# Unread matmuls in shorter pauses of TensorE, placed nearer to the next step

## The chip, the cores and the metric

The kernel runs on one core of one Trainium2 chip. The metric is the time of one execution on the device in microseconds; lower is better. All times in this text are from this kernel on that chip. Times of the profile are counted from the start of its span.

## The reference

The input x has 8 sequences of 1024 rows of 256 numbers. Four stages follow each other, each with a residual sum around it and a layer norm in front:

1. A linear attention layer with 16 heads of width 16: q and k are sigmoids of projections, two rounds of running sums over the sequence give the flows that scale them, and kv is a running sum of outer products. A projection, a layer norm, a dense layer of width 1024 with GELU and a second layer norm belong to the stage.
2. A dense layer of width 1024 with ReLU.
3. Softmax attention over the whole sequence with width 256.
4. A gated feed-forward layer of inner width 704 whose inputs and weights are first rounded, in blocks of 16, to a grid of eight magnitudes (FP4) times a scale per block.

Cut to its last lines:

```python
    x = x + _L0_attn_ref(_layernorm(x, axis=-1), ...)
    x = x + _L0_ffn_ref(_layernorm(x, axis=-1), ...)
    x = x + _L1_attn_ref(_layernorm(x, axis=-1), ...)
    x = x + _L1_ffn_ref(_layernorm(x, axis=-1), ...)
```

All matmuls are in float32; one such matmul stands in the trace as two passes, each with its own weight load. A transpose against the identity is one pass.

## The kernel before, in words

The work is cut into 64 chunks of 128 rows. Four chunks are a group, two groups a sequence, so there are 16 groups p. `linear_group` (L998) and `linear_span` (L1061) do the linear attention of a group, `dense` (L1451) the two dense layers, `soft_chunk` (L1620) the softmax attention and the FP4 layer of one chunk, `fp4_weights` (L787) the rounding of the weights. A chunk is turned by `flip` (L683) either on TensorE against the identity or by a copy on GpSimd (`cut`), a transposing DMA (`spun`) and a copy on ScalarE. Group 0 goes through TensorE, and in its case in two halves.

Each of these functions is a Python generator. It yields what its next step needs (an engine, tiles, a number of PSUM banks) and issues instructions when it is resumed. All generators lie in one list, and `Plan.run` (L330) chooses which one goes on. The order of instructions on every engine is then fixed as the order in which they were issued. So the program's order is set at build time by estimates of time:

- `Plan.took` (L176) holds a cost for each operation, and books when its engine is free again and when each tile is ready and last used. For TensorE it also books `ran`, the estimated end of the last matmul (L246). A pause of over 2.0 us in the estimates doubles the cost of the matmuls of the next 2.1 us (L242 to L246).
- `Plan.ready` (L298) answers when the step's engine is free and when its tiles and banks are there. `banks_free` (L126) tells from when on a number of the 8 PSUM banks can be had.
- `Plan.run` takes the step with the smallest key: first how long TensorE would wait for it, last its place in the plan (due times from the table `T` at L31).
- When the chosen step is TensorE's and the estimates leave a pause on TensorE before it, `run` may call `fill` (L1774). It takes one PSUM bank and issues products of the identity with itself into it. Nobody reads them. Their number is set at build time; on the chip they stand in TensorE's queue like any matmul, and what stands behind them waits until they are done. The first of them can run only when GpSimd has made the identity (`make_identity`, L497).

In the kernel before, such products are put where the estimated pause is over 1.6 us and a bank is free within 0.4 us of the pause's start; their estimated length is the pause less 0.7 us, at 0.22 us each. The estimate of the first pause counts from 0, since `ran` starts at 0 (L110).

All instructions are issued through one helper (L376), so the profile shows L376 for nearly all of them. They are told apart by their tiles: `bank<-ident` are the unread products, `bank<-ident,n` and the like are transposes.

Of the kernel before, what the change touches and what calls it, by code (L numbers as in the profile page):

```python
# [75 lines left out]
class Plan:  # L76
# [253 lines left out]
    def run(self):  # L330
        while self.parts:
            now = self.free.get("tensor", 0.0)
            best = None
            for part in self.parts:
                t = self.ready(part[1])
                if t is None:
                    continue
                stays = self.tiled and part[1].tiled
                queue = part[1].queue
                wait = max(max(t) - now - (0.3 if stays or part[2] < 0.0 else 0.0), 0.0)  # L340
                urgent = part[2] < 0.0
                unripe = 0.0 if urgent else max(t[1] + self.RIPE[queue] - now, 0.0)
                key = wait, unripe, queue == "tensor", not stays, part[2]
                if best is None or key < best[0]:
                    best = key, part, max(t)
            assert best is not None, "every part waits for another"
            pause = max(now, best[2]) - self.ran
            if pause > 1.6 and best[1][1].queue == "tensor" and self.fill is not None:
                if (self.banks_free(best[1][1].banks + 1) or 0.0) <= self.ran + 0.4:
                    self.fill(pause - 0.7)  # L350
            if best[0][0] > 0.0 or best[1][1].queue == "tensor":
                self.free["tensor"] = max(now, best[2])
            part = best[1]
            need = next(part[0], None)
            if need is None:
                self.parts.remove(part)
            else:
                part[1] = need
                if need.at is not None:
                    part[2] = need.at  # L360
# [34 lines left out]
def block_stack_kernel(ctx: ExitStack, tc: tile.TileContext, a: dict, out: bass.AP):  # L395
# [20 lines left out]
    plan = Plan(tc, tc.nc)  # L416
# [16 lines left out]
    def mm_bank():  # L433
        bank = ps.tile([P, 512], F32, tag="bank", name="bank")
        plan.bank(bank)
        return bank
# [1334 lines left out]
            )  # L1771
            plan.start(soft_chunk(cc), T["soft"] + min(cc, B * NCH - T["tail"]) / 4)

    def fill(us):  # L1774

        bank = mm_bank()
        while us > 0.0:
            nc.tensor.matmul(bank[:, :P], lhsT=ident, rhs=ident, start=True, stop=True)
            us -= 0.22
        plan.let_go(bank)  # L1780

    plan.fill = fill
# [45 lines left out]
```

## Time and profile before

| What | us |
|---|---|
| median of 3 timed runs | 2479.97 (2478.25 to 2480.6) |
| the profiled execution | 2475.61 |
| its span, first to last instruction | 2473.9 |
| TensorE (PE) busy | 2431.3 |
| VectorE (DVE) busy | 1893.8 |
| ScalarE (ACT) busy | 1397.6 |
| GpSimd (POOL) busy | 1233.7 |
| unread products: 310 passes, busy | 39.6 |

PE is TensorE's matmul row and PEld its weight loads. Matmuls are pipelined, so that a row's end is modelled and reaches some 0.16 us into the row that follows it back to back. A row of the timeline gives start, length, engine, line, operation, output and inputs, shape and number; brackets behind it give the idle time of that engine just before, and what ended it. The mean granted clock of TensorE is 0.996 of full speed over the span.

### The profile page before, as it was taken

Reading aid. Unit: us, or ns where it says so; the run is one execution under the profiler, and the core shown is the slowest. Engines: PE = TensorE matmul, PEld = TensorE weight load, DVE = VectorE, ACT = ScalarE, POOL = GpSimd, SP = SyncE. Lnnn points to the kernel's source line nnn. Section 1 sums busy time; section 2 is a strip of 40 time slices with the busy share of each in tenths; the row PEclk is TensorE's granted clock in tenths of the full one; section 3 lists DMA queues with packets and bytes.
Section 4 is the critical chain, followed back from the end, with each engine's and each line's share of the span. In section 5 each row is a group of like instructions: output and inputs, shape, how many; then the busy total and the mean of one; then the engine's idle time right before and its main releaser. Section 6 shows DMA issues by size and latency. Waiting matters only on the chain.

```text
span 2473.9 us, 47678 instructions
## 1 busy us (share of the span) xinstructions
PE 2431.3 (98%) x16503; PEld 1896.0 (77%) x16503; DVE 1893.8 (77%) x4139; ACT 1397.6 (56%) x2913; POOL 1233.7 (50%) x2257
## 2 busy tenths in 40 slices
PE   8899999999999999999999999999999999999998
PEld 6787777777777777777777777777777777777766
DVE  6877687967868788786977878787786877766777
ACT  5444556465565556656466565555556555555454
POOL 3354546454554646455563555546455464544342
PEclk9999999999999999999999999999999999999999
DMA  3265455555455556564555465556554655555242
GB/s 103 71 155 155 125 145 129 143 139 137 114 122 150 130 128 145 131 133 121 149 137 129 114 151 127 129 136 131 134 137 125 145 119 130 126 122 131 68 83 56
DMA packets 630354, 312.62 MB, mean 126 GB/s; under 512 B 433760, under 2 KB 618592, under 8 KB 630112
## 3 DMA queue, kind: packets, MB, share of 16 engines
q1 hardware_dynamic: 630112, 309.57, 51.5%
q8 instruction: 131, 2.15, 0.4%
q14 instruction: 111, 0.91, 0.1%
HBM read 188.17 MB, written 20.71 MB: 84 GB/s over the span
## 4 chain that ended last, share of the span: by engine, by line
PE 88%; DVE 7%; DMA 2%; ACT 1%; POOL 1%; issue 1%; SPq 0%; DVEq 0%; ACTq 0%; POOLq 0%
PE bank L376 88%; DMA spun<-cut 1%; DVE hid L376 1%; DVE prod L376 1%; DVE u L376 0%; DVE n L376 0%; DVE ln_st L376 0%; DVE x_amax L376 0%; POOL ln_rstd L376 0%; DVE w_raw L376 0%; DVE res L376 0%; POOL cut L376 0%; DVE div L376 0%; POOL ln_shift L376 0%; DVE ln_mv L376 0%
## 5 line engine op out<-in xcount | busy, mean ns | idle before, releaser
L376 PE MATMUL bank<-half,w_in 128*128 128x256 f32 x2048 | 532.2, 383 | 12.5 <-ACT half L376 7.9
L376 PE MATMUL bank<-w_out,hidden 128*128 128x256 f32 x2048 | 524.3, 384 | 2.6 <-DMA w_out<-in_L_attn_W_dram 1.9
L376 PEld LDWEIGHTS bank<-w_out,hidden 128*128 128x128 f32 x2048 | 378.0, 190 | 104.5 <-issue 46.3
L376 PEld LDWEIGHTS bank<-half,w_in 128*128 128x128 f32 x2048 | 385.8, 191 | 83.7 <-issue 13.2
L376 POOL TENSOR_SCALAR ln_ve<-ln_mv 128x1 f32<-128x1 f32 x384 | 101.3, 264 | 560.8 <-DVE ln_mv L376 520.9
L376 ACT ACTIVATE hidden<-bank,c_L_attn_b 128x256 f32<-128x256 f32 x256 | 120.2, 470 | 242.7 <-PE bank L376 242.4
L376 ACT ACTIVATE hidden<-bank,c_L_ffn_b 128x256 f32<-128x256 f32 x256 | 121.1, 473 | 236.8 <-PE bank L376 235.4
L376 POOL TENSOR_TENSOR ln_rstd<-ln_ve,neghalf 128x1 f32<-128x1 f32 x384 | 232.3, 605 | 32.0
L376 PE MATMUL bank<-n2T,qT 128*128 128x512 f32 x512 | 242.0, 596 | 2.5 <-ACT qT L376 2.5
L376 PE MATMUL bank<-vt,probT 128*128 128x256 f32 x1024 | 231.9, 379 | 0.0
L376 POOL COPY cut<-n 128x512 uint16<-128x512 uint16 x238 | 170.9, 726 | 96.7 <-DVE n L376 58.0
L376 PEld LDWEIGHTS bank<-vt,probT 128*128 128x128 f32 x1024 | 193.5, 190 | 31.9 <-issue 5.3
L376 POOL COPY cut<-hid 128x512 uint16<-128x512 uint16 x165 | 117.6, 736 | 154.3 <-DVE hid L376 133.9
L376 POOL COPY cut<-prob 128x512 uint16<-128x512 uint16 x218 | 145.7, 691 | 93.9 <-ACT prob L376 54.2
L376 PE MATMUL bank<-wdT,hqT 128*128 128x256 f32 x768 | 177.3, 380 | 1.8 <-ACT hqT L376 1.8
L376 PE MATMUL bank<-wgT,xqT 128*128 128x352 f32 x512 | 173.9, 462 | 1.6 <-ACT xqT L376 1.2
L376 PE MATMUL bank<-wuT,xqT 128*128 128x352 f32 x512 | 172.4, 459 | 0.0
L376 ACT COPY probT<-spun 128x512 uint16<-128x512 uint16 x246 | 159.2, 673 | 19.9 <-DMA spun<-cut 19.6
L376 ACT ACT_TABLE_LOAD x128 | 164.2, 1283 | 3.7 <-PE bank L376 1.5
L376 PEld LDWEIGHTS bank<-wdT,hqT 128*128 128x128 f32 x768 | 144.8, 190 | 26.9 <-ACT hqT L376 3.2
L376 PEld LDWEIGHTS bank<-n2T,qT 128*128 128x128 f32 x512 | 97.0, 191 | 74.7 <-issue 59.2
L376 PEld LDWEIGHTS bank<-wuT,xqT 128*128 128x128 f32 x512 | 97.3, 190 | 54.2
(274 smaller groups left out, 4808.1 us busy)
## 6 DMA issues: line engine op xcount, KB each, us to landing
w_in<-in_L_attn_W_dram SPq DMA_DIRECT2D x128, 256.0 KB
w_out<-in_L_attn_W_dram SPq DMA_DIRECT2D x128, 256.0 KB
w_in<-in_L_ffn_w_dram SPq DMA_DIRECT2D x128, 256.0 KB
w_out<-in_L_ffn_w_dram SPq DMA_DIRECT2D x128, 256.0 KB
spread<-packed SPq DMA_DIRECT2D x90, 256.0 KB
spun<-cut SPq DMA_TRANSPOSE x767
x<-in_L_attn_inputs_dram SPq DMA_DIRECT2D x64, 128.0 KB
xr<-in_L_attn_inputs_dram SPq DMA_DIRECT2D x64, 128.0 KB
```

The source lines that it names most:

```text
L376: ins = method(*args, **kw)
```

## The change

Three things in `run` and `fill`:

- Products are now put into estimated pauses of over 0.9 us, before 1.6 us.
- They are to end 0.4 us before the next step, before 0.7 us. `fill` gets this point in time in place of a length, and `run` sets `ran` to it.
- While nothing has run on TensorE (`ran` is 0), the pause is counted from 2.4 us on, and a product is reckoned as 0.36 us. Else it is reckoned as 0.22 us, as before.

The condition on the bank is the same. The estimates in `took` are the same, but each product passes through them, so the planner's later choices could differ.

```diff
-            pause = max(now, best[2]) - self.ran
-            if pause > 1.6 and best[1][1].queue == "tensor" and self.fill is not None:
+            until = max(now, best[2])
+            if until - self.ran > 0.9 and best[1][1].queue == "tensor" and self.fill is not None:
                 if (self.banks_free(best[1][1].banks + 1) or 0.0) <= self.ran + 0.4:
-                    self.fill(pause - 0.7)
+                    self.fill(until - 0.4)
+                    self.ran = until - 0.4
             if best[0][0] > 0.0 or best[1][1].queue == "tensor":
                 self.free["tensor"] = max(now, best[2])
...
-    def fill(us):
+    def fill(until):
 
         bank = mm_bank()
+        us = until - (plan.ran or 2.4)
+        each = 0.22 if plan.ran else 0.36
         while us > 0.0:
             nc.tensor.matmul(bank[:, :P], lhsT=ident, rhs=ident, start=True, stop=True)
-            us -= 0.22
+            us -= each
         plan.let_go(bank)
```

## The prediction

> **What bounds the kernel now.** The page's first view gives the busy shares, its fourth the chain that ended last. I then read TensorE's own timeline for its pauses, the windows view for the granted clock beside them, and the two built programs' orders of instructions for where products come and go.
>
> ```profile
> PE 2431.3 (98%) x16503; PEld 1896.0 (77%) x16503; DVE 1893.8 (77%) x4139; ACT 1397.6 (56%) x2913; POOL 1233.7 (50%) x2257
> ...
> PE 88%; DVE 7%; DMA 2%; ACT 1%; POOL 1%; issue 1%; SPq 0%; DVEq 0%; ACTq 0%; POOLq 0%
> ```
>
> TensorE is the chain for 88% of the span and stands idle for only 2473.9 - 2431.3 = 42.6 us. So a product that nobody reads is free only inside a real pause; between two matmuls that already follow each other it is paid in full. A fill can earn time in two ways only: TensorE starts earlier, or its clock stays up.
>
> The orders show what the diff becomes. There were 155 unread products in 13 places; there are 240 in 30. The first place falls from 25 to 10; the others grow from 130 to 230, that is 100 more. All other TensorE instructions keep their order, SP and POOL are the same, and DVE and ACT differ by one or two neighbours exchanged, which I price at nothing. No DMA is moved. One product is two passes; 28 passes from 2452.31 to 2455.44 give 0.112 us each, so **0.223 us a product** at full clock.
>
> **Part 1, the start.** TensorE's and DVE's timelines:
>
> ```profile
> 3.10 8.46 PE L376 MATMUL bank<-ident 128*128 128x128 f32 x50 [3.10 <-POOL ident masks.py:199]
> 11.39 0.60 PE L376 MATMUL bank<-ident,n 128*128 128x128 f32 x4
> ...
> 7.22 0.41 DVE L376 TENSOR_SCALAR n<-x,ln_mv,ln_rstd 128x256 f32<-128x256 f32 x1 [0.44 <-POOL ln_rstd L376]
> ...
> 11.66 0.18 DVE L376 BATCH_NORM_AGGREGATE ln_mv<-ln_st 128x2 f32<-128x6 f32 x1
> 14.18 0.69 DVE L376 TENSOR_TENSOR_SCAN prod<-one,k 128x256 f32<-128x256 f32 x1 [2.34 <-ACT k L376]
> ```
>
> The second normalised chunk is ready at 7.22 + 0.41 = 7.63, but its transposes wait behind 50 unread passes until 11.39. Seen from 5.60 on, 39 passes are left, so 11 took 2.50 us (0.227 each, half clock); 20 passes then end at 3.10 + 20 x 0.227 = 7.6. The transposes go some 3.7 us earlier. What is late next is DVE: it runs without a pause until 11.66 + 0.18 = 11.84, and its scan, which waited 2.34 us for ACT's k, can start there and not sooner. Later DVE waits on ACT (0.17, 0.90 us) give back a little more. I take **-2.6**; bounds -1.0 (the 16 passes of wk and wq at half clock, 16 x 0.22 = 3.5 us more, partly inside the 1.56 us of fill that follows them) and -3.5.
>
> **Part 2, the clock.** The windows view, laid at the edges where the granted clock changes:
>
> ```profile
> 30.40:35.90 5.50, 1.93 (x21) 1.11 (x20) 4.68 (x11) 2.08 (x9) 2.90 (x4) 1.00 0.08 25
> 35.90:42.73 6.83, 5.77 (x8) 2.47 (x9) 3.69 (x7) 3.10 (x7) 0.72 (x1) 0.50 0.44 114
> 114.41:117.82 3.41, 1.52 (x28) 1.05 (x29) 3.19 (x9) 1.77 (x3) 1.36 (x2) 1.00 0.00 0
> 117.82:121.23 3.41, 3.41 (x10) 2.75 (x9) 1.46 (x5) 3.27 (x9) 0.00 (x0) 0.50 0.03 7
> 209.98:213.39 3.41, 1.36 (x6) 1.24 (x7) 3.12 (x11) 0.95 (x3) 2.33 (x6) 1.00 0.52 121
> 213.39:216.81 3.42, 3.42 (x9) 2.72 (x9) 2.41 (x6) 1.31 (x4) 1.72 (x4) 0.50 0.66 199
> 247.53:250.94 3.41, 2.02 (x18) 1.82 (x16) 3.24 (x12) 1.60 (x5) 1.06 (x4) 1.00 0.92 202
> ```
>
> Columns: stretch, length, busy time of PE, PEld, DVE, ACT, POOL, granted clock, DMA. After a stretch in which PE was busy 35 to 45% (1.93 of 5.50, 1.52 and 1.36 of 3.41) the next one has half the clock; after 59% (2.02 of 3.41) it has not. At 612.75 to 616.17 (0.61 of 3.42) the fourth such spell begins.
>
> *The spell at 35.90.* Four passes of n2T,wk take 3.78 us there and 1.88 at 46.77; those of wq 2.63 and 1.98; the transposes before 0.69 and 0.44. Together 1.90 + 0.65 + 0.25 = 2.8. Behind them DVE stands:
>
> ```profile
> 39.41 0.28 DVE L376 TENSOR_TENSOR scale<-e,div 64x128 f32<-64x128 f32 x1
> ...
> 45.05 0.75 DVE L376 TENSOR_TENSOR q<-q,bank 128x256 f32<-128x256 f32 x2 [4.70 <-PE bank L376]
> ```
>
> Scale is ready at 39.69 and TensorE reaches it at 43.79, so 2.8 fit into those 4.1. Nine new products (2.0 us) lie before the hsum and total matmuls; they bring the stretch to (1.93 + 2.0)/5.50 = 71% busy. I take **-2.8**, bounds 0 and -2.8.
>
> *The spell at 213.39.* Five products go into the 2.37 us pause before 212.03: (1.36 + 1.12)/3.41 = 73%. The 12 passes from 212.03 take 3.98 us to the next start; at 0.216 (four in 0.86 at 1164.66) they take 2.6. **-1.4**, bounds 0 and -1.4; the DMA that follows (w_in, released by the last of them) moves with it.
>
> *The other spells.* No fill is put before the one at 616.17, and in front of 117.82 only 2 products are added, ahead of the pauses. I leave both. The 2.82 us pause at 249.5 gets 6 more products; it caused no spell here, so on the profiled execution it earns nothing.
>
> A rule weighed against this: the Trainium skill, "TensorE: Matmul & The Clock Gate", section "HAM oscillation — how this bites in real kernels", tells writers to avoid idle gaps of over about 3.4 us. By it no pause of this kernel needs a fill, both spells would stay, and the sum below would be +4.8. The rows above speak against it: the pauses before the spells were 2.37 us and less, and what they share is a low busy share. Its section "What's actually happening" says that the 3413 ns window runs free, which agrees with the 3.41 and 6.83 us lengths here.
>
> **Part 3, products in front of ready work.** Two places from TensorE's timeline:
>
> ```profile
> 1164.66 1.03 PE L376 MATMUL bank<-half,w_in 128*128 128x256 f32 x4
> 1165.52 1.03 PE L376 MATMUL bank<-w_out,hidden 128*128 128x256 f32 x4
> ...
> 2349.94 0.81 PE L376 MATMUL bank<-ident,prob 128*128 128x128 f32 x4
> 2351.47 1.98 PE L376 MATMUL bank<-n2T,qT 128*128 128x512 f32 x4 [0.71 <-ACT qT L376]
> ```
>
> Six products go between the first two, which have no pause: +1.34. The others on the chain: 5 at 121.6 (+1.12); 3 at 160.6, where 0.25 us was idle (+0.42); 5 at 696.3 (+1.12); 3 at 739.8 (+0.67); 5 at 2338.7 and 4 at 2350.8, 2.01 less the 0.71 idle (+1.30); 5 at 2447.1, in front of the last wgT matmuls whose result DVE's last chunk waits for (+1.12). That is 36 products, less the two pauses: **+7.1**. From 616 to 1354 the chain is TensorE without a break, so nothing there absorbs them. The rest is covered and I take **+0.3** for all: 1 to 6 more each at 16, 18, 26.7, 62.5, 98, 105, 110, 133.6, 219.2, 252, 279, 338, 1527, 2424, 2452 and 2459, where TensorE at its next waits stands for 0.2 to 2.8 us (on DVE, ACT or DMA), and 4 each at 61 and 2467 in pauses of 0.2 to 0.6 us. If that cover were gone, their price would be the remaining 100 - 36 - 9 - 5 = 50 products, +11 us. Lower bound for all of part 3: half, +3.7, if DVE has slack behind some of them.
>
> **Sum** against the profiled execution (2475.6 us, span 2473.9): -2.6 - 2.8 - 1.4 + 7.1 + 0.3 = +0.6. That execution is 4.4 us under the median of the timed runs (2479.97). Two or three more spells of 3.41 us at half clock, 1.7 us each, would make such a difference, and a pause causes one or not by where it falls in the window. The pause at 249.5 would cause one in about 6 of 10 executions (it must leave some 1.8 us of a 3.41 us window idle); filled, that is -1.0 against the median. Forecast: 2480.0 + 0.6 - 1.0 = **2479.6**.
>
> **Rivals.** *Faster.* The start gains 3.5, the spell at 117.82 falls away too with the changed phase (-1.7), and half of part 3 is absorbed by DVE's slack: -3.5 - 2.8 - 1.4 - 1.7 - 1.0 + 3.7 = -6.7, 2473.3. For it: DVE is busy 77% and has stretches of its own on the chain (598 to 616, 1354 to 1378). Against it: PE's timeline has no idle time over 0.2 us from 620 to 1378, so there is no slack to take from.
>
> *Slower: the fills do not hold the clock.* If the new products around 32 to 36 us leave a free-running window below about half busy, the spell there stays, and fills inside it cost double. Then parts of 2 give 0, the 5 products at 121.6 lie in a half-clock spell (+1.1) and the total is -2.6 + 7.4 + 1.1 = +5.9, 2485.9. It decides at a busy share between the 45% that lost the clock and the 59% that kept it; the 1.23 us pause before 36.50 stays unfilled, so a window around it can come to about 50%.
>
> *The change does nothing measurable at its places* (each fill exactly replaces idle time, the clock as before) is inside the forecast's range.
>
> **How the numbers follow.** Bounds of the parts, not all at once: low -6.7, high +5.9. Chances: forecast 0.66, the faster rival 0.21, the slower one 0.13. 0.2% is 5.0 us, about what a measurement of this kernel can tell from no change. The range that should hold 8 in 10 goes from 2473.4 to 2485.4; the forecast's own is 2475 to 2485.
>
> **What would show it.** Right: 20 unread passes from 3.10 and transposes by 8; DVE's first scan near 11.9; a granted clock of 1.00 from 36 to 43 and n2T,wk in some 1.9 us; no spell after the pause that was at 209.7; and rows of 6 to 12 unread passes at about 690, 735 and 1160 with no idle time before or after. Wrong: wk at half clock after the start, the 6.83 us spell still there, or an idle pause of TensorE right after a fill in the steady part, which would mean that the fill cost nothing. The forecast fails if the clock gains and the product costs do not come to nearly the same size, or if an unread product waits for its bank.

## The result, and the profile after

| | before | after |
|---|---|---|
| median of the timed runs, us | 2477.89 (12 runs, 2472.9 to 2480.6) | 2485.91 (12 runs, 2483.9 to 2489.2) |
| the profiled execution, us | 2475.61 | 2485.57 |
| its span, us | 2473.9 | 2483.9 |
| PE busy, us | 2431.3 | 2448.4 |

The change makes the kernel slower: 1.0039 of the time before, with a 95% interval of 1.0031 to 1.0047. By the medians that is +8.0 us. The forecast was no measurable change. Its starting point, 2480.0, was the median of three runs; the 12 runs here put the kernel before 2.1 us lower. The page of the changed kernel, busy time and chain:

```profile
PE 2448.4 (99%) x16673; PEld 1915.3 (77%) x16673; DVE 1892.9 (76%) x4139; ACT 1397.0 (56%) x2913; POOL 1234.6 (50%) x2257
...
PE 88%; DVE 6%; DMA 1%; POOL 1%; ACT 1%; issue 1%; SPq 0%; POOLq 0%; DVEq 0%; ACTq 0%
```

TensorE stands idle for 2483.9 - 2448.4 = 35.5 us, 7.1 less than before, and yet the span is 10.0 longer: busy time rose by 17.1. The 85 more products at 0.223 us make 19.0, so all other work together changed by only -1.9. A higher busy share is no gain when the work that raises it is unread.

The first transposes went as forecast. PE's timeline after:

```profile
3.10 4.21 PE L377 MATMUL bank<-ident 128*128 128x128 f32 x20 [3.10 <-POOL ident masks.py:199]
7.15 0.38 PE L377 MATMUL bank<-ident,n 128*128 128x128 f32 x2
```

They start at 7.15 in place of 11.39. Then the windows view, laid at the edges of the granted clock (stretch, length, busy time of PE, PEld, DVE, ACT, POOL, clock, DMA share, GB/s):

```profile
34.03:37.44 3.41, 1.71 (x9) 0.98 (x9) 2.56 (x6) 2.00 (x7) 1.85 (x2) 1.00 0.16 44
37.44:40.85 3.41, 3.41 (x5) 1.37 (x5) 2.18 (x5) 1.41 (x3) 0.00 (x0) 0.50 0.70 110
218.35:221.76 3.41, 0.59 (x3) 0.57 (x4) 3.31 (x8) 0.19 (x1) 2.54 (x3) 1.00 0.92 248
221.76:225.17 3.41, 3.41 (x10) 2.66 (x9) 0.10 (x1) 0.96 (x2) 2.20 (x4) 0.50 0.03 6
252.48:255.89 3.41, 0.89 (x6) 0.65 (x6) 3.06 (x9) 1.50 (x5) 2.96 (x6) 1.00 1.06 267
255.89:259.31 3.42, 3.42 (x17) 2.29 (x19) 0.00 (x0) 2.30 (x6) 2.24 (x6) 0.50 0.19 38
```

The spell of half clock near 36 us is half as long, the one at 213.39 is gone, and there are two new ones, at 221.76 and 255.89. Each follows a stretch in which PE waited (0.59 and 0.89 us busy of 3.41). PE's timeline says for what:

```profile
209.86 1.28 PE L377 MATMUL bank<-ident 128*128 128x128 f32 x10
211.11 2.86 PE L377 MATMUL bank<-half,w_in 128*128 128x256 f32 x12
...
216.40 1.28 PE L377 MATMUL bank<-ident 128*128 128x128 f32 x10
221.17 1.47 PE L377 MATMUL bank<-half,w_in 128*128 128x256 f32 x4 [3.49 <-DMA w_in<-in_L_attn_W_dram]
```

The fill at 209.86 closes the pause and the 12 passes behind it take 2.86 us, as forecast. But the next w_in matmul waits 3.49 us for its transfer and starts at 221.17, where the kernel before started it at 220.96. In this trace the gain is given back inside 5 us. In the steady part the fill stands between matmuls that follow each other:

```profile
1171.12 1.03 PE L377 MATMUL bank<-half,w_in 128*128 128x256 f32 x4
1171.98 1.50 PE L377 MATMUL bank<-ident 128*128 128x128 f32 x12
1173.32 1.03 PE L377 MATMUL bank<-w_out,hidden 128*128 128x256 f32 x4
```

There is no bracket before or behind it: 1173.32 - 1171.98 = 1.34 us, paid in full, the figure of the forecast.

One table carries most of what follows. It gives, for single passes of PE, how much later (+) or earlier (-) the same pass starts than in the kernel before, in the one profiled execution of each kernel (the columns are the pass's time before):

| kernel | 11.4 | 116 | 206.4 | 216.9 | 221.0 | 224 | 252.4 | 256 | 600 | 1600 |
|---|---|---|---|---|---|---|---|---|---|---|
| the change | -4.24 | -1.72 | +0.37 | -2.60 | +0.21 | +1.89 | +2.93 | +4.15 | +4.52 | +8.03 |
| start only | -3.86 | -2.11 | -0.44 | -3.40 | -0.24 | +1.28 | +2.62 | +3.64 | +3.68 | +4.63 |
| first 500 us only | -3.92 | -3.35 | -1.94 | -4.91 | -2.49 | -0.81 | +1.16 | +2.23 | +2.19 | +4.34 |
| 18 products first | -2.52 | -2.25 | -1.99 | -1.89 | -2.65 | -2.65 | -2.49 | -0.09 | -0.29 | -0.80 |
| 33 products first | +0.57 | +0.82 | +0.86 | -2.11 | +0.35 | +1.91 | +2.12 | +3.33 | +4.43 | +5.30 |
| start, long fills | -3.87 | -1.84 | -0.75 | -2.10 | -0.72 | -0.79 | -0.63 | -0.69 | +0.52 | +1.34 |
| before, long fills | -0.41 | -0.38 | -0.50 | -2.12 | -0.71 | -0.71 | +0.64 | +0.64 | +0.50 | +1.52 |
| start, fill at 221 | -3.86 | -0.36 | -0.27 | -1.42 | -0.03 | -0.10 | +0.02 | +0.02 | +2.65 | +2.66 |
| change, long fills | -4.10 | -3.96 | -0.49 | -3.46 | -0.52 | -0.52 | +1.25 | +1.24 | +0.94 | +5.44 |

Read the first row from left to right: 2.60 us in front at 216.9, 0.21 behind at 221.0, 4.15 behind at 256. Of the 10.0 us by which this span is longer, 3.8 arise between 206 and 256, where the change has 23 products (5.1 us), each group at the start of a pause; another 3.5 arise between 600 and 1600.

### The profile page after: what moved, and what is told of

It reads as the page before. It is cut to its first block, busy times and chain, and to the rows that moved or that the text cites. A ratio compares the mean times of both kernels' runs of the same rounds, so it can differ in the third digit from the quotient of the medians.

```text
span 2483.9 us, 48024 instructions
## 1 busy us (share of the span) xinstructions
PE 2448.4 (99%) x16673; PEld 1915.3 (77%) x16673; DVE 1892.9 (76%) x4139; ACT 1397.0 (56%) x2913; POOL 1234.6 (50%) x2257
## 4 chain that ended last, share of the span: by engine, by line
PE 88%; DVE 6%; DMA 1%; POOL 1%; ACT 1%; issue 1%; SPq 0%; POOLq 0%; DVEq 0%; ACTq 0%
PE bank L377 88%; DMA spun<-cut 1%; DVE prod L377 1%; DVE hid L377 1%; DVE n L377 1%; DVE ln_st L377 0%; DVE u L377 0%; DVE k L377 0%; POOL ln_rstd L377 0%; DVE x_amax L377 0%; POOL cut L377 0%; DVE w_raw L377 0%; POOL ln_shift L377 0%; DVE res L377 0%; DVE ln_mv L377 0%
## 5 line engine op out<-in xcount | busy, mean ns | idle before, releaser
L377 DVE TENSOR_TENSOR sc<-bank,tri 128x384 f32<-128x384 f32 x240 | 118.5, 545 | 27.6 <-PE bank L377 26.7
```

What stands on the lines that cost most here:

```text
L377: ins = method(*args, **kw)
```

## The experiments

Each was compared with the kernel before on the same chip (three chips in all, with medians of 2477.95, 2477.31 and 2477.1 for the kernel before). In each, products alone differ; the order of all other instructions of PE, SP and POOL was left as it was, but for the last one. Differences are given as medians in us and as the record's ratio with its 95% interval. The ratio is not the quotient of the two medians: for the change it means +9.7 us where the medians say +8.0, and further down the two differ by up to 1.2 us. An argument that hangs on 1 or 2 us is therefore not safe.

**First round.** Two theories of the loss. *A:* the products in front of ready work make it, and the gains of the early part are absorbed on the way. *B:* the early part itself loses, by new or moved spells of half clock and pauses. The change's rule was applied to parts of the program by one condition in `run`, and the rule before elsewhere:

```diff
-            pause = max(now, best[2]) - self.ran
-            if pause > 1.6 and ...
+            until = max(now, best[2])
+            new = self.ran == 0.0      # start only
+            new = until < 500.0        # first 500 us only
+            new = until >= 500.0       # after 500 us only
+            if until - self.ran > (0.9 if new else 1.6) and ...
```

*Start only.* 

> Only the first fill is as in the change (10 products, 20 passes); all others are as before. Theory A (products in front of ready work make the loss, and the earlier start is swallowed on the way by GpSimd's small operations and by the transposing DMAs): the transposes go 4 us earlier, the first hsum matmuls 1.7, the transposes at 31 us 0.7; against before -0.3 to -1.0 us. Rival B (the early part costs: the start or the moved pauses bring new spells at half clock): +1 to +4 us. The step as predicted: -2.6 us.

Measured: 2482.35, +4.4 us, 1.0019 (1.0011 to 1.0028). Fifteen products fewer than before, and slower by over half of what the change loses. That is B's direction, just above its range, and against the prediction's -2.6.

*First 500 us only.* 

> The change's rule up to 500 us of the plan, the rule of before after that; no new products in the steady part or at the end. Theory A: early costs of about 2.5 us (5 products at 121 us, 2 at 134 us, part of 6 at 284 us) less at most 2 us of gain: 0 to +3 us against before. Rival B: nearly all of the loss is here, +6 to +8 us.

Measured: 2481.24, +3.3 us, 1.0014 (1.0005 to 1.0022). Between the two; the prediction's steps for this part add up to about -6.

*After 500 us only.* 

> The rule of before up to 500 us of the plan, start included, the change's rule after that. Theory A: 5, 3, 6 and 3 products in the stretch from 696 to 1527 us and those from 2338 us on are paid nearly in full, +5 to +6.5 us against before. Rival B: the products lie where something else is late, 0 to +2 us.

Measured: 2481.19, +3.2 us, 1.0014 (1.0005 to 1.0023). Also between the two. The loss has two halves, and neither theory had it alone.

*The products of the steady part doubled* (the whole change, 30 in place of 17 products between 500 and 2300 us):

```diff
-            us -= each
+            us -= each / (2.0 if 500.0 < until < 2300.0 else 1.0)
```

> The change, with the four fills between 500 and 2300 us made longer, from 17 products to 30 (9, 5, 11 and 5). 13 more products at 0.223 us. Theory A: 2.4 to 2.9 us more than the change, that is +10.5 to +11 us against before. Rival B: no more than the change, +8 us.

Measured: 2489.65, +11.7 us, 1.0048 (1.0036 to 1.0060), above A's range. Over the change that is 3.7 us by the medians and 2.2 by the ratios, for 13 products that come to 2.9. The late half is A's: such a product costs about its full length.

**Second round: why does an earlier start lose?** In the run with the start alone, SP's and PE's timelines show this around 212 us:

```profile
212.26 3.15 SPq L379 DMA_DIRECT2D spread<-packed  x4
215.46 1.10 SPq L379 DMA_DIRECT2D w_in<-in_L_attn_W_dram  x2
```

```profile
210.31 2.86 PE L379 MATMUL bank<-half,w_in 128*128 128x256 f32 x12 [1.09 <-ACT half L379]
...
220.72 2.05 PE L379 MATMUL bank<-half,w_in 128*128 128x256 f32 x4 [4.96 <-DMA w_in<-in_L_attn_W_dram]
...
254.99 2.08 PE L379 MATMUL bank<-half,w_in 128*128 128x256 f32 x4 [4.12 <-ACT half L379]
```

and in the kernel before:

```profile
213.42 2.51 SPq L376 DMA_DIRECT2D spread<-packed  x4
215.97 2.73 SPq L376 DMA_DIRECT2D w_in<-in_L_attn_W_dram  x2
```

```profile
220.96 1.10 PE L376 MATMUL bank<-half,w_in 128*128 128x256 f32 x4 [1.80 <-DMA w_in<-in_L_attn_W_dram]
```

Without the spell at 213, PE is through sooner and waits 4.96 us instead of 1.80 for the same landing; 4 passes then take 2.05 us at half clock. Theory *C:* a PE that comes early lets the loads collide, waits, and loses the clock. Rival *P:* the loss is in proportion to the start. Two runs shift the start, two lengthen the fills in the pauses at 212, 221 and ahead of 252 us:

```diff
+        if not plan.ran:
+            us = 0.22 * 17.5           # 18 products first; 32.5 for 33
```

```diff
+        if plan.ran and 200.0 < until < 262.0:
+            us = 0.22 * {0: 5, 1: 15, 2: 21}.get(held[0], 0) - 0.1
+            held[0] += 1
```

*18 products first.* 

> The kernel before, with 18 products in the first fill instead of 25 (the change has 10). Theory C (collision): TensorE that is early at 212 us frees the buffers of w_in and w_out early, these loads are issued together and share the DMA engines with the four spread loads, so the w_in that is awaited at 221 lands no sooner, TensorE pauses 3 us or more there and loses the clock, and the same again at 252. 7 products of 0.42 us less put TensorE forward by up to 2.9 us at the start, of which about 1.7 us should be left at 212, as in the run with 10 products, so: +2 to +4.5 us, with spells at half clock at 220 to 222 and 254 to 256. Rival P (proportion): a start that is earlier by x is worth 0.6x, and the loss of the run with 10 products is one of the start's own: -1.0 to -1.8 us, with no new spells.

Measured: 2478.57, +1.3 us, 1.0009 (1.0001 to 1.0018). Neither by the medians; the ratio's +2.2 us would be in C's range, but the spells are not where C put them: they start at 211.38 and 248.93.

*33 products first.* 

> The kernel before, with 33 products in the first fill instead of 25: TensorE later by 8 products of 0.42 us, 3.4 us at the start. Theory C: at 212 TensorE is at most some 1 to 2 us later, the loads are issued later and apart, and no spell appears at 221 or 255; the waits for transfers at 221 and 252 (0.5 and 3.5 us in the kernel before) take the delay up: -1 to +1.5 us. Rival P: +1.5 to +2 us, in proportion.

Measured: 2480.96, +3.6 us, 1.0018 (1.0009 to 1.0027). Neither: a later start loses almost as much as an earlier one. (The kernel before waits 1.80 us at 221 and 2.82 at 252 in its trace, not 0.5 and 3.5.) PE's timelines, first of the run with 18, then with 33 products, show what the two have in common with the others:

```profile
210.14 4.31 PE L379 MATMUL bank<-half,w_in 128*128 128x256 f32 x12 [2.47 <-ACT half L379]
...
218.31 1.10 PE L379 MATMUL bank<-half,w_in 128*128 128x256 f32 x4 [1.04 <-DMA w_in<-in_L_attn_W_dram]
```

```profile
211.61 2.86 PE L379 MATMUL bank<-half,w_in 128*128 128x256 f32 x12 [1.09 <-ACT half L379]
...
221.31 2.04 PE L379 MATMUL bank<-half,w_in 128*128 128x256 f32 x4 [4.25 <-DMA w_in<-in_L_attn_W_dram]
```

With 18 the pause at 210 is 2.47 us, the 12 passes run largely at half clock (4.31 us), and the wait behind them is short, as in the kernel before. PE is still 2.49 us in front at 252.4; that is gone by 256, in the spell of 6.83 us that starts at 248.93. With 33 the pause is 1.09 us, the passes are quick, the wait is 4.25 us, and the next passes run at half clock, as in the change. So C's "early" was wrong. The reading of these traces: what decides is whether PE loses its clock **in front of** the w_in wait, where it costs nothing since PE would wait anyway, or **behind** it, where it counts. The next runs test it.

*Start only, with the long fills.* 

> The run with 10 products in the first fill alone, and in the three pauses at 212, 221 and 252 us 5, 15 and 21 products (the change has 5, 5 and 13; the kernel before none, none and 7), long enough to last until the awaited transfer. Theory C with the clock: the two spells of 3.41 us at half speed that follow the pauses at 221 and 252 go, each had given some 1.2 to 1.4 us, so +4.4 falls to about +1.6 us (bounds +0.5 to +2.5); what is left is the later landing. Rival T (transfers alone): what follows waits for transfers anyway, and the spells only fill waits: +3.5 to +5 us.

Measured: 2475.16, -2.1 us, 0.9996 (0.9987 to 1.0005). From +4.4 to about nothing, by 34 more unread products.

```profile
216.90 3.51 PE L379 MATMUL bank<-ident 128*128 128x128 f32 x30
220.24 1.03 PE L379 MATMUL bank<-half,w_in 128*128 128x256 f32 x4
...
247.05 4.85 PE L379 MATMUL bank<-ident 128*128 128x128 f32 x42
251.74 1.07 PE L379 MATMUL bank<-half,w_in 128*128 128x256 f32 x4
```

The w_in matmul starts 0.48 us sooner, at 220.24, but its 4 passes take 1.03 us in place of 2.05, and PE is at 252 in time. The recovery is more than the two spells: against the run with the start alone, the pass of 252.37 is 3.25 us sooner (-0.63 against +2.62), before the second spell could act. About 0.9 of it is a transposing DMA ahead of 252, which reached the copy that reads it 3.81 us after its issue in place of 4.75.

*The kernel before, with the long fills.* 

> The kernel before with its 25 products at the start, and 5, 15 and 21 products in the pauses at 212, 221 and 252 us. Theory C: the spell at 213 goes and TensorE comes to 221 some 2.6 us earlier, as in the change, the loads collide, w_in lands no sooner, but no spell follows: -1.5 to +1.5 us. If the collision alone is enough, without the clock (rival T): +2.5 to +4.5 us, with TensorE late at 252 by 2 us or more.

Measured: 2477.59, +0.3 us, 1.0003 (0.9995 to 1.0012). C's range: PE is 2.12 us in front at 216.9, 0.71 at 221, and nothing is won or lost, though the spell at 213 is gone.

**Third round.** Theory *S:* the spell behind the 221 wait is also what makes PE late at 252. Rival *T:* the transfers collide by themselves.

*Start only, long fill at 221, but 7 products ahead of 252* (`2: 7` in the edit above). 

> The run with 10 products in the first fill, 5 in the pause at 212 and 15 in that at 221, but in the pause ahead of 252 us the 7 of the kernel before instead of 21. Theory S (the spell at half speed after the pause at 221 is what makes TensorE late at 252): without that spell the pass at 252.37 of the kernel before comes no later than there, and only a spell of 1 to 1.3 us behind the pause ahead of 252 is left: -1 to +1.5 us. Rival T (the transfers collide by themselves): TensorE is at 252 later by 2 us or more, as in the run with the start alone: +2 to +4.5 us.

Measured: 2478.89, +1.8 us, 1.0009 (1.0000 to 1.0017). Its time lies between the theories; its PE timeline does not:

```profile
247.89 1.73 PE L379 MATMUL bank<-ident 128*128 128x128 f32 x14
252.40 1.13 PE L379 MATMUL bank<-half,w_in 128*128 128x256 f32 x4 [2.78 <-ACT half L379]
...
335.30 2.94 PE L379 MATMUL bank<-w_out,hidden 128*128 128x256 f32 x8 [2.64 <-DMA w_out<-in_L_attn_W_dram]
```

With no spell at 221, PE is at 252.40 against 252.37 in the kernel before, as S says. But S is not the whole of it: with the long fills, the kernel before, the change and the first 500 us have no spell at 221 either, and yet PE falls back by 1.35, 1.77 and 1.60 us from 221 to 252. There the copy behind the second transposing DMA comes 4.93, 4.76 and 4.75 us after its issue, here 3.68. So part of the lateness at 252 is T's. The 2.78 us pause ahead of 252 cost no clock this time. The +2.65 us of the table came at 335, in a wait for w_out with 6.83 us of half clock from 336.14 on, where nothing had been edited.

*The whole change, with the long fills.* 

> The whole change, with 15 products instead of 5 in the pause at 221 us and 21 instead of 13 in that ahead of 252, so that they last until the awaited transfers. Theory S: the two spells at 221 and 255 go, and with them 4.5 to 6.5 us of the change's loss, as between the runs of the start without and with these fills; left are the products in front of ready work after 500 us, which were +3.2 us alone: +1.5 to +4 us over the kernel before. If the loss of the change has its cause elsewhere (products in front of ready work alone, or the transfers), it stays at +7 to +9 us.

Measured: 2481.31, +4.2 us, 1.0015 (1.0006 to 1.0024). That is at the edge of S's range and far below +7 to +9: 18 more unread products take back half of the loss or more. What is left is about the +3.2 us of the products after 500 us. PE's timeline shows that the fill did not quite reach the transfer, and that the clock held all the same (4 passes in 1.10 us):

```profile
215.54 3.51 PE L377 MATMUL bank<-ident 128*128 128x128 f32 x30
220.44 1.10 PE L377 MATMUL bank<-half,w_in 128*128 128x256 f32 x4 [1.39 <-DMA w_in<-in_L_attn_W_dram]
```

*First 500 us only, with the long fills.* 

> The change up to 500 us alone, with 15 and 21 products in the pauses at 221 and ahead of 252 us instead of 5 and 13, and the rule before after 500 us. Theory S: +3.3 us less 4.5 to 6.5 us: -1 to -3 us against the kernel before. Otherwise +2.5 to +4.5 us.

Measured: 2478.32, +1.2 us, 1.0000 (0.9992 to 1.0009). In the right direction (+3.3 before), but not the gain that S forecast. The spells at 219 and 253 are gone; this trace has others at 115.07 and 336.93 (3.41 us each), and the one near 616, which most traces have, lasts 6.83 us here.

*Why does w_in not land sooner?* The run with the start alone, but with the four spread loads ahead of w_in cut to a quarter:

```diff
             nc.sync.dma_start(
-                out=t,
+                out=t[:, :cut_to],
...
-                    ap=[[GT, 16], [0, DH // 2], [1, GT]],
+                    ap=[[GT, 16], [0, DH // 2], [1, cut_to]],
```

> The run with 10 products in the first fill alone, but the four spread loads at 212 us bring a quarter of the columns (64 KB each instead of 256 KB; the missing columns are not computed rightly, VectorE multiplies by the first quarter instead). The order of TensorE's instructions is the same up to the w_in matmul at 221; behind it the planner's order differs, so only this landing is read, not the time. If w_in lands late because it shares the DMA engines with the spread loads, 768 KB less at 248 GB/s are up to 3.1 us: w_in's matmul starts near 218 us instead of 220.72, after a wait of some 2 us instead of 4.96. If w_in is late for its own sake (its issue, its own bytes), the matmul starts at 220.2 or later.

SP's timeline and PE's:

```profile
213.68 3.10 SPq L379 DMA_DIRECT2D spread<-packed  x4
216.83 1.10 SPq L379 DMA_DIRECT2D w_in<-in_L_attn_W_dram  x2
```

```profile
219.98 1.10 PE L379 MATMUL bank<-half,w_in 128*128 128x256 f32 x4 [2.81 <-DMA w_in<-in_L_attn_W_dram]
```

By the clock time of the expectation (218 against 220.2) this falls near the second answer, but this execution was 1.4 us later already at 212 (the one execution of this kernel took 2490.8 us, which says nothing here, as its order differs behind 221). What counts is from the issue of w_in to its matmul: 219.98 - 216.83 = 3.15 us, against 220.72 - 215.46 = 5.26 with the full loads, and the wait is 2.81 against 4.96. So in this one execution some 2.1 us of the landing go with the bytes in front of it, the answer that the shared DMA engines would give, and not the 3.1 of the estimate. The rest of its time is its place: w_in is issued at the end of the spread loads' issue (212.26 + 3.15 = 215.41), and those read `packed`, which is filled from a flow that VectorE has just made. Across the traces with full loads in which PE waits for it, the matmul starts 4.65 to 5.51 us after the issue (after 500 us only 4.65, 18 products 4.98, before 4.99, 33 products 5.03, first 500 us 5.14, start only 5.26, change 5.51), whether PE is there early or not.

**The clock over all runs.** A trace is one execution, but the record lists the mean granted clock of every run. In the traces the clock is either full or half, so a run's time at half clock is 2 x (1 - mean clock) x span. The averages, good to about 1 us (for the kernel before, over its runs beside the experiments):

| kernel | mean clock | us at half clock |
|---|---|---|
| before (89 runs) | 0.9956 | 21.5 |
| the change | 0.9965 | 17.4 |
| start only | 0.9945 | 27.5 |
| first 500 us only | 0.9968 | 15.7 |
| after 500 us only | 0.9963 | 18.5 |
| 18 products first | 0.9946 | 26.6 |
| 33 products first | 0.9946 | 26.6 |
| start, long fills | 0.9964 | 18.0 |
| before, long fills | 0.9973 | 13.5 |
| start, fill at 221 | 0.9952 | 23.9 |
| change, long fills | 0.9981 | 9.5 |
| first 500 us, long fills | 0.9977 | 11.3 |

A spell can cost at most half its length. The long fills take 9.5, 7.9 and 4.4 us of half clock out of the start alone, the change and the first 500 us, worth up to 4.8, 4.0 and 2.2 us. The loss against the kernel before falls by 6.5, 3.8 and 2.1 us by the medians (5.7, 5.9 and 3.5 by the ratios). Out of the kernel before they take some 8 us, worth up to 4, and its time does not fall. So over all runs, and not in single traces only, half clock at these places cost about its full price or more in the changed kernels, and next to nothing in the kernel before (unless the fills there cost as much as they won, which was not tried apart). What goes beyond the full price is not the clock's own. And the change as a whole spends less time at half clock than the kernel before, and is slower all the same.

**Which pause loses the clock?** The steady-part run has the change's program up to 500 us, and in its trace PE waits 3.46 us at the same place, after 3.49 in the change. It keeps the clock:

```profile
223.66 1.10 PE L377 MATMUL bank<-half,w_in 128*128 128x256 f32 x4 [3.46 <-DMA w_in<-in_L_attn_W_dram]
```

The spells of a trace lie on one grid of 3.41 us. The windows view on that grid, first of this run, then of the kernel before, of the start with long fills and of the change with long fills (columns as above):

```profile
218.60:222.01 3.41, 1.60 (x13) 1.35 (x11) 2.97 (x6) 0.98 (x3) 1.47 (x4) 1.00 0.93 226
222.01:225.43 3.42, 1.77 (x8) 1.62 (x9) 2.30 (x4) 0.57 (x2) 3.00 (x4) 1.00 0.55 187
```

```profile
332.86:336.27 3.41, 1.68 (x8) 1.44 (x8) 3.27 (x10) 2.68 (x6) 0.00 (x0) 1.00 0.82 202
336.27:339.68 3.41, 1.67 (x8) 1.25 (x7) 3.34 (x6) 3.36 (x8) 1.95 (x2) 1.00 0.84 266
```

```profile
333.09:336.51 3.42, 1.46 (x7) 1.33 (x8) 3.28 (x9) 2.08 (x6) 0.00 (x0) 1.00 1.20 225
```

```profile
109.43:112.84 3.41, 1.80 (x36) 0.95 (x34) 3.26 (x7) 0.77 (x2) 2.25 (x3) 1.00 0.00 0
```

In the steady-part run a window's edge cuts the wait, each half leaves its window about half busy, and no spell follows; in the change 2.8 us of it lie in one window, which is 17% busy. Behind the windows of the kernel before (49% busy) and of the start with long fills (43%) the clock stayed full; behind that of the change with long fills (53%) it fell. Over all 14 traces, from 13 us on, every window at full clock with PE busy for under 42% was followed by half clock and none over 53% was; between the two there are both. So the same pause costs the clock or not by where the grid lies in that execution.

## Why the prediction was wrong

**The sum failed in parts 1 and 2, not in part 3.** The gains of 6.8 us that it took off the profiled execution, and the 1.0 against the median, did not come; the cost of 7.4 did, roughly. The step that failed is the price of a spell: the sum took every slow stretch that a fill removes as time won at the end, and did not ask what ends the next wait. Less half clock did come (17.4 us in place of 21.5 over all runs), but not less time.

- *Part 1, the start, -2.6.* The first effects were right: transposes at 7.15 (forecast 7.6), DVE's scan at 12.07 (11.84), and 1.7 to 2.1 us still in hand at 116. The failing step is that this lead was taken as lasting to the end. At 206 the change is at +0.37, of which 8 products in front of ready work at 121.6 and 160.6 are +1.5, and the run with the start alone, which has none of these, at -0.44: its spell at 114.57 lasted 6.83 us in place of 3.41. At 221 nothing is left, and that run is +4.4 by the medians. Where the spell near 115 is missing, as in the trace of the first 500 us alone, 1.94 us are in hand at 206 and 2.49 at 221. So the lead is not lost to one cause, and why that spell comes shorter, longer or not at all was not tried apart.
- *Part 2, the spell at 35.90, -2.8.* The fill brought the window from 34.03 to 37.44 to 1.71/3.41 = 50% busy, and the clock fell all the same; the spell came to 3.41 us in place of 6.83. Of the 2.8 it took, 1.1 came: from the transposes ahead of n2T,wk to scale it is 7.29 us before and 6.23 in the change. The prediction reckoned the share over the 5.50 us between two changes of the clock (71%), not over the 3.41 us window that counts. The slower rival's border, a share between 45% and 59%, is not sharp: windows between 43% and 53% went either way. In the traces of the first 500 us alone and of the change with long fills, the same instructions up to here ran with no such spell: one program, different windows. There (first 500 us) the stretch takes 4.53 us, so the size of 2.8 was right and the certainty was not.
- *Part 2, the spell at 213.39, -1.4.* **This is the step that failed worst.** The 12 passes did get quicker, 2.70 us in place of 3.98. But the prediction read "the DMA that follows (w_in, released by the last of them) moves with it". It does not: the w_in that PE waits for next stands behind the four spread loads in SP's queue, is issued at 215.97 before and at 215.66 in the change, and its matmul starts about 5 us after that. The pause of 2.37 us and the spell at 213 lay in the shadow of that landing. In the change 3.0 us are won between 206 and 216.9, and lost again by 221.0, and PE, now idle instead of slow, loses its clock behind the wait: +1.7 by 224, then +1.0 up to 252 and +1.2 in a second spell. The runs with 18 and 33 products show the two patterns, and the long fills remove the second. Of the +1.0 up to 252, some may be the transposing DMA's and not the spell's (see the third round).
- *Part 2, the pause at 249.5, -1.0.* It was filled with 13 products, 3.07 us long, and PE still waited 2.52 us behind them, since the copy that it waits for came later; a spell followed. Two of the premises were off as well. By the condition given (1.8 of 3.41 us idle), a pause of 2.82 us fails only when a window's edge cuts it between 1.02 and 1.80 us, so it would lose the clock in about 8 of 10 executions and not 6. And the 4.4 us to the median, which was to be two or three spells, was 2.3 with 12 runs; the runs' mean clock of 0.9956 against 0.9964 in the profiled one is about one spell.
- *Part 3, +7.1 and +0.3.* Its mechanism held: six products at 1171.98 cost 1.34. The part after 500 us, 5.6 us in the forecast, gave +3.2 alone by medians, and 13 more products gave 2.2 to 3.7. In the trace of the change PE falls back by 3.5 us from 600 to 1600, where the forecast had 3.1 (1.12 + 0.67 + 1.34). That agreement is loose: traces without a new product in this stretch change by -0.5 to +2.2 us there. So the size was right or somewhat high.
- *The slower rival* gave 2485.9, which is the measured time, by luck: it was +5.9 on a start of 2480.0, and +8.0 on 2477.9 was measured. It was right that the fills did not hold the clock at 36. It had the 5 products at 121.6 at half clock, and they cost 1.20 us, their length at full clock. At 213 the fill did hold the clock, and the early loss comes behind that. The rival lacked the spells at 221 and 255.
- *The rule that was weighed* ended nearer than the rows did, with its sum of +4.8, but not for its reason: the spell at 213 did go. Waits of 3.10 us (first 500 us), 3.49 (change), 4.25 (33 products) and 4.96 (start only) at 221 were followed by half clock, the one of 3.46 in the steady-part run was not. The Trainium skill, "TensorE: Matmul & The Clock Gate", section "HAM oscillation — how this bites in real kernels", describes just this: a wait for a transfer longer than the window, and a cold start behind it. These runs agree with it for the waits of 3.49 us and more; but it isn't the whole rule, since the wait of 3.46 us kept the clock and pauses of 2.37 and 2.47 us lost it.

The change's loss of 8.0 us is thus about +3.3 from the first 500 us and +3.2 from the rest when tried apart; the remaining 1.5 (2.7 by the ratios) is within the intervals of the three. Of the +3.3, the long fills take back 2.1.

**What stays open.** Each kernel has one trace, and spells differ between executions of the same instructions, so a single spell is no property of a kernel; the medians and mean clocks over 11 or 12 runs are (5 for the steady-part run). What sets the border between 43% and 53% is open. Why the second transposing DMA ahead of 252 takes from 3.7 to 5.7 us from its issue to the copy that reads it was not tried apart. Nor was why the pause at 212 is 2.4 to 2.6 us long in some traces and 1.1 in others. No version was clearly faster than the kernel before: the start with the long fills comes nearest, with an interval that holds 1.

## What to carry to other kernels

Before a slow or idle stretch is priced as a gain, follow the next wait behind it to its issue: if a transfer that does not start sooner ends that wait, the stretch is free as it is, and removing it only turns slow work into a longer pause. Where a pause must exist, unread work helps if what is left of the pause behind it is short: here 1.39 us kept the clock, and some 3.5 us lost it in one trace and kept it in another. The clock is lost at the pause's end, in front of work that counts. In places where the engine follows on without a pause, each unread product costs its full length, whatever the planner estimated there.

## What the runs showed of the hardware

- Over 14 traces, a 3.41 us window of the grid with PE under 42% busy at full clock was always followed by half clock, one over 53% never; 49% kept it in the kernel before, 50% lost it in the change. After pauses of 2.4 to 2.8 us it was lost in some traces (2.37 before, 2.47 with 18 products) and kept in others (2.82 before and 2.78 with the fill at 221, both ahead of 252).
- Spells come at other places in executions of the same instructions: 37.44 and 115.95 in the trace of the change, 112.84 alone (6.83 us) up to 600 us in that of the change with long fills, none up to 219 in that of the first 500 us alone. The 3.41 us grid does not start with the program.
- A half-clock spell can cost nothing: without the one at 213 PE was 1.7 us further ahead at 216.9 than at 212, and at 221 nothing of it was left; over all runs, some 8 us less half clock in the kernel before with long fills changed its time by +0.3 us. Behind the wait it counts: with the start alone, PE lost 1.5 us between 221.0 and 224.
- Four transfers of 256 KB in front of a fifth cost it 2.1 us of landing time more than four of 64 KB, in one execution of each.
